# Two key products on VectorE and the slots' denominators on TensorE, in a four-layer graph kernel

## The chip, the core and the metric

One core of a Trainium2 chip runs the whole kernel. Its engines work side by side, each through its own queue in order: TensorE (PE, matrix products into PSUM), VectorE (DVE), ScalarE (ACT), GpSimd (POOL, which also issues the indirect DMAs here) and SyncE (SP, which issues the other DMAs). They wait for one another through semaphores. The metric is the device time of one execution in microseconds; shown times are medians of several runs.

## The reference, cut to what matters

Four layers over N = 2708 nodes with 128 channels, each added to its input after a layer norm and a ReLU. The change lies in layer 1, the attention:

```python
q = (x @ Wq.T).reshape(d, n, h)          # d = 128 slices, n = 2708 nodes, h = 8
k = (x @ Wk.T).reshape(d, n, h)
v = (x @ Wv.T).reshape(d, n, h)
a = jnp.einsum('dnh,dmh->dnm', q, k) * scale
a = a + spatial_encoding + edge_encoding   # both are adj: a sparse matrix, 1 to 16 entries in a row
a = jax.nn.softmax(a, axis=2)
out = jnp.einsum('dnm,dmh->dnh', a, v)
```

A softmax over all 2708 nodes, for each of 128 slices, with a sparse term added to the logits.

## The kernel before, in words

The kernel splits the softmax in two parts. **The dense part** is without adj: the exponential of a small logit is written as a cubic polynomial in the products of the eight coordinates of q and k, so that sums over all nodes become small matrix products of features. **The sparse part** is a correction for each node's neighbours, with weight exp(logit) times (exp(2 adj) - 1).

**Dense part.** Slices are taken in 64 pairs, d = 0 to 63, and each pair in six chunks of node tiles, c = 0 to 5 (`chunks`, L1515; 4, 4, 3, 4, 4 and 3 tiles of 22). In one pass of the loop over c (L1624):

- `turn` (L1519) transposes the query features of the next chunk on TensorE into `f_ps`, ScalarE copies them to `fT`.
- `evaluate` (L1530) multiplies them with the moments `mw` into `g_ps` on TensorE; VectorE multiplies by the last coordinates into `z` (L1546) and reduces into `o_raw` (L1555).
- `queries(d + 1)` makes the next pair's query features in `fq` on VectorE (L802, helper `mul_v`): p0, p1, p2 at c = 1, xy at c = 2, t0 and t1 at c = 3, t2 and the norms at c = 4.
- `moments(d + 1)` multiplies the key features `fk` with the values `y` on TensorE into `m_ps` (L869), c = 0 to 4; `weighted` (L877) makes `mw` of them at c = 5.
- `keys(d + 2)` makes key features in `fk` on GpSimd (L805, helper `mul_g`): p0, p1, p2 at c = 1, xy (16 products per node and slice) at c = 2, t0 (10 products) at c = 3, t1, t2 and the norms at c = 4. `with_values(d + 2)` multiplies keys with values into `y`, on GpSimd, at c = 3 and c = 5.

The query features read their coordinates from `kq_ps`, a copy in PSUM; the key features read `kv_t`, a copy in SBUF.

**Sparse part.** At the end of each pass the loop also advances a chain of generators, `first` (L1422): by slices, then sorting of the rows, then `from_neighbours` (L1211), in which nodes stand sorted by their number of neighbours in 22 tiles of 128, and tile t has `ROOM[t]` slots (16, 9, 8, ... 2; 121 in all). A slot b takes one neighbour of each of 128 nodes:

- `load`: an indirect DMA from GpSimd's queue gathers the neighbours' keys and values into `c_kv`, two slots ahead, in a ring of five buffers
- `logits` (L1246): GpSimd multiplies keys by queries, in place
- `summed` (L1252): VectorE reduces over the eight coordinates into `c_c`, in PSUM; two slots alternate in `c_two`
- `weigh` (L1258): ScalarE takes the exponential and scales by the weight, in place; for a tile's first slot it also copies the result to `c_den`
- `values` (L1269): VectorE multiplies values by weights into `c_v`; for later slots it then adds the weights to `c_den` (L1282)
- `added` (L1284): TensorE adds `c_v` into `v_ps` with two products by the identity
- `copied_out` (L1301), `store`: at a tile's end ScalarE copies sums and denominators out, and an indirect DMA stores them

`from_neighbours` yields six times per slot. In one round it does, with a yield between: load of slot b+2 and values of b-2; logits of b; summed of b-1; added of b-2; weigh of b-1; copied_out. `faster()` (L1417) sets four yields per chunk when this stage begins. So a pair (six chunks, 24 yields) takes exactly four slots, and the places where they fall into the six chunks are the same in every pair. The instructions are issued in the order in which the code runs (`manual_schedule`); only the waits are added by the framework.

After the stage the rest of `first` is gone, and the loop goes on with normalising and the output projection beside the remaining pairs.

Of the kernel before, what the change touches and what calls it, by code (L numbers as in the profile page):

```python
# [9 lines left out]
FP = mybir.dt.float32  # L10
AF = mybir.ActivationFunctionType
ALU = mybir.AluOpType
# [4 lines left out]
P = 128  # L17
BF = mybir.dt.bfloat16
BK = 512
HEAD = 8  # L20
# [7 lines left out]
ROOM = (16, 9, 8, 7, 7, 7, 6, 6, 6, 5, 5, 5, 5, 4, 4, 4, 4, 3, 3, 3, 2, 2)  # L28
# [10 lines left out]
LIN, XX, YY, XY, YYY, F_END = 1, 5, 15, 25, 41, 61  # L39
# [7 lines left out]
def gnn4_kernel(  # L47
# [22 lines left out]
    nc = tc.nc  # L70
    N, C = x.shape
# [19 lines left out]
    ident = const.tile([P, P], FP, name="ident")  # L91
# [114 lines left out]
    with ExitStack() as ph:  # L206
# [56 lines left out]
        with tc.manual_schedule():  # L263
# [108 lines left out]
            for i, t in enumerate(order):  # L372
                r0, sz = rows[t]
# [6 lines left out]
                d = dinv[:sz, t : t + 1]  # L380
# [100 lines left out]
            for t in range(STAY, NT):  # L481
# [3 lines left out]
                sz = rows[t][1]  # L485
# [78 lines left out]
    most2 = keep.tile([P, 2, C], FP, name="most2")  # L564
# [168 lines left out]
    parts = [(0, NT // 2), (NT // 2, NT)]  # L733
    TM = max(b - a for a, b in parts)

    def features(mul, k, k2, f, most):

        T = k.shape[1]
        n = k.shape[0]
        gs = k[:, :, :HEAD].rearrange("p t (g e) -> p t g e", g=2)  # L740
        hs = k2[:, :, :HEAD].rearrange("p t (g e) -> p t g e", g=2)
        two = f[:, :, XX : XX + 20].rearrange("p t (g w) -> p t g w", g=2)
        yy = f[:, :, YY : YY + 10]

        def pair(e, o):
            w = 3 - e
            mul(
                two[..., o : o + w],
                gs[..., e : e + 1].to_broadcast([n, T, 2, w]),
                hs[..., e + 1 : 4],  # L750
            )

        def triple(o, left, right):
            w, v = left.shape[2], right.shape[2]
            if v == 1:
                mul(f[:, :, o : o + w], left, right.to_broadcast([n, T, w]))
            else:
                mul(
                    f[:, :, o : o + w * v].rearrange("p t (a b) -> p t a b", a=v),
                    left[:, :, None].to_broadcast([n, T, v, w]),  # L760
                    right[:, :, :, None].to_broadcast([n, T, v, w]),
                )

        def norms_of():
            n2 = early.tile([P, 2 * NT], FP, name="n2", bufs=2)
            nc.vector.tensor_reduce(n2, two[..., 3:7], axis=AX.XY, op=ALU.add)
            nc.vector.tensor_reduce(
                most, n2.rearrange("p (t i) -> p i t", i=2), axis=AX.X, op=ALU.max
            )

        return {
            "sq": lambda: nc.scalar.activation(two[..., 3:7], gs, AF.Square),  # L772
            "lin": lambda: nc.scalar.copy(f[:, :, LIN : LIN + 4], k[:, :, 4:8]),
            "p0": lambda: pair(0, 0),
            "p1": lambda: pair(1, 7),
            "p2": lambda: pair(2, 9),
            "xy": lambda: triple(XY, k2[:, :, 0:4], k[:, :, 4:8]),
            "t0": lambda: triple(YYY, yy, k[:, :, 4:5]),
            "t1": lambda: triple(YYY + 10, yy[:, :, 4:], k[:, :, 5:6]),
            "t2": lambda: triple(YYY + 16, yy[:, :, 5:7], k[:, :, 6:8]),  # L780
            "n": norms_of,
        }
# [31 lines left out]
    fks, fqs, fts, pms, mws, ros = {}, {}, {}, {}, {}, {}  # L814

    copied, turned_ = {}, {}

    def of_pair(d, at):
        i = 2 * (d % (GRP // 2))
        return got[d // (GRP // 2)][:, i : i + 2, :, at]  # L820

    def flat(a):
        return a.rearrange("p t i k -> p (t i) k")
# [6 lines left out]
    def keys(d):  # L830

        kv = early.tile([P, NT, 2, QKV - HEAD], FP, name="kv_t", bufs=KV_BUFS)
        nc.scalar.copy(kv.rearrange("p t i k -> p i t k"), of_pair(d, slice(HEAD, QKV)))  # L833
        turned_[d] = kv = flat(kv)
        fks[d] = fkp[d % 2]
        return features(mul_g, kv, kv, flat(fks[d]), most2[:, 1, 2 * d : 2 * d + 2])

    def with_values(d, h):

# [52 lines left out]
    def opening():  # L892
# [23 lines left out]
        for part in (queries(0), keys(1)):  # L916
            yield from whole(part)
# [8 lines left out]
    with ExitStack() as ph:  # L926
# [10 lines left out]
        with tc.manual_schedule():  # L937
# [10 lines left out]
            for t, (r0, sz) in enumerate(rows):  # L948
# [4 lines left out]
                for i in range(3):  # L953
                    scale = (C**-0.5, 1.0, 1.0)[i]
                    for c0 in (0, HALF):
# [5 lines left out]
                            start=True,  # L961
                            stop=True,
# [112 lines left out]
    with ExitStack() as ph:  # L1075
# [3 lines left out]
        sm = ph.enter_context(tc.tile_pool(name="l1_sm", bufs=2, reuse_waits="tile"))  # L1079
# [5 lines left out]
        ps_c = ph.enter_context(tc.tile_pool(name="l1_psc", bufs=1, space=PSUM, reuse_waits="tile"))  # L1085
# [123 lines left out]
        S = 1  # L1209

        def from_neighbours():  # L1211
# [4 lines left out]
            nc.vector.tensor_scalar_add(cw, cw, -1.0)  # L1216
            todo = [(t, s0, w) for t in range(NT) for s0, w in _cuts(ROOM[t], S)]
            qs, kvs, cs, accs, dens = {}, {}, {}, {}, {}
            c_two = ps_c.tile([P, 2, S, C], FP, name="c_c")
            done = []  # L1220

            def load(b):
# [35 lines left out]
            def weigh(b):  # L1258

                t, s0, w = todo[b]  # L1260
                sz = rows[t][1]
                c = cs[b][:sz]
                nc.scalar.activation(c, c, AF.Exp)  # L1263
                nc.scalar.activation(c, c, AF.Copy, scale=cw[:sz, t, s0 : s0 + 1])
                if s0 == 0:
                    dens[t] = sm.tile([P, C], FP, name="c_den")
                    nc.scalar.copy(dens[t][:sz], c)

            def values(b):  # L1269
                t, s0, w = todo[b]  # L1270
                sz = rows[t][1]
                c, kv = cs.pop(b)[:sz], kvs.pop(b)
                vs[b] = z = tm.tile([P, 2, BK // HEAD, HEAD], FP, name="c_v", tag="c_v")
                nc.vector.tensor_tensor(  # L1274
                    z[:sz],
                    kv[:sz, 0, :, 1].rearrange("p (j c) k -> p j c k", j=2),
                    c.rearrange("p (j c) -> p j c", j=2)[:, :, :, None]
                    .to_broadcast([sz, 2, C // 2, HEAD]),
                    ALU.mult,
                )  # L1280
                if s0:
                    nc.vector.tensor_tensor(dens[t][:sz], dens[t][:sz], c, ALU.add)  # L1282

            def added(b):  # L1284
                t, s0, w = todo[b]
                sz = rows[t][1]
                z = vs.pop(b)
                if s0 == 0:
                    accs[t] = ps_v.tile([P, 2, BK], FP, name="v_ps")
                for j in range(2):  # L1290
                    nc.tensor.matmul(  # L1291
                        accs[t][:sz, j],
                        ident[:sz, :sz],
                        z[:sz, j].rearrange("p c k -> p (c k)"),
                        start=s0 == 0,
                        stop=s0 == ROOM[t] - 1,
                    )
                if s0 + w == ROOM[t]:
                    done.append(t)

            def copied_out():  # L1301
                while done:
                    t = done.pop()
                    sz = rows[t][1]
                    acc = nkv[t % 2].rearrange("p t c -> p (t c)")[:, : C * VW].rearrange(
                        "p (c k) -> p c k", k=VW
                    )
                    nc.scalar.copy(
                        acc[:sz, :, :HEAD],
                        accs.pop(t)[:sz].rearrange("p j (c k) -> p (j c) k", k=HEAD),  # L1310
                    )
                    nc.scalar.copy(acc[:sz, :, HEAD], dens.pop(t)[:sz])
                    ready.append((t, acc))

            def store():
# [47 lines left out]
        def unit_of(g):  # L1363
            return g // 2 if g < NG - 2 else g - NG // 2 + 1
# [52 lines left out]
        def faster():  # L1417

            pace[0] = 4.0
            yield  # L1420

        first = chain(by_node(), sorted_rows(), faster(), from_neighbours())  # L1422
        beside = []
        done = 0
# [34 lines left out]
            return ps_v.tile([P, 2, BK], FP, name="v_ps")  # L1459

        def sum_bank():
            return ps_c.tile([P, 2, S, C], FP, name="c_c")[:, 0, 0]

        def projected(t, ring):

# [148 lines left out]
        with tc.manual_schedule():  # L1614
# [7 lines left out]
            for d in range(D):  # L1622
                asked, keyed = {}, {}
                for c in range(NCH):  # L1624
# [32 lines left out]
                    while owed >= 1 and first is not None:  # L1657
                        owed -= 1
                        if next(first, "done") == "done":
                            first = None  # L1660
                    if first is None:
                        owed = 0
                        for _ in range(4):
                            step(n, unit_of(max((d - 1) // PG, 0)))
                        if d < D - 1:
                            normalising()
# [34 lines left out]
    with ExitStack() as ph:  # L1701
        with ExitStack() as gh:
# [7 lines left out]
            with tc.For_i(0, once):  # L1710
                with tc.For_i(0, C) as d:
# [5 lines left out]
                    q, k, v = nat  # L1717
# [5 lines left out]
                    o = gp.tile([P, NT, HEAD], FP, name="g_o")  # L1723
# [105 lines left out]
        with tc.tile_pool(name="l2_pa", bufs=1, space=PSUM) as pa, tc.manual_schedule():  # L1829
# [3 lines left out]
            for i, t in enumerate(in_turn):  # L1833
                sz = rows[t][1]
# [10 lines left out]
                for c, (c0, cw) in enumerate(cols):  # L1845
                    nc.tensor.matmul(
                        pgs[c][:, :cw], h2[:sz, t], a[:sz, c0 : c0 + cw],
                        start=i == 0, stop=i == NT - 1,
# [29 lines left out]
        with tc.tile_pool(name="l3_g4", bufs=NC) as g4, tc.tile_pool(  # L1878
            name="l3_ln", bufs=2, space=PSUM
# [121 lines left out]
    with ExitStack() as ph, tc.manual_schedule():  # L2001
        gp = ph.enter_context(tc.tile_pool(name="l3_g", bufs=4, reuse_waits="tile"))
        zp = ph.enter_context(tc.tile_pool(name="l3_z", bufs=2, reuse_waits="tile"))
        sm = ph.enter_context(tc.tile_pool(name="l3_sm", bufs=3))
# [58 lines left out]
    with tc.tile_pool(name="l3_more", bufs=2) as mp, tc.tile_pool(  # L2063
        name="l3_once", bufs=1
# [7 lines left out]
        with tc.For_i(0, nc.values_load(ovf, min_val=0, max_val=1)):  # L2072
# [13 lines left out]
            most = mp.tile([P, 1], FP, name="most")  # L2086
# [10 lines left out]
            with tc.For_i(0, rounds):  # L2097
                for t, (r0, sz) in enumerate(rows):
# [11 lines left out]
                    f = mp.tile([P, 8], FP, name="col_f")  # L2110
# [76 lines left out]
```

## Time and profile before

| | us |
|---|---|
| median of 3 runs (2151.46 to 2160.33) | 2151.55 |
| the profiled execution | 2157.09 |
| its span in the trace | 2155.3 |
| slots of neighbours, first load to last `v_ps` product | about 743 to 1471 |

Busy time over the whole span: TensorE 1692.6 us (79%), VectorE 1444.2 (67%), GpSimd 1321.0 (61%), ScalarE 931.8 (43%). These shares are means over stages with different limits; what the change is worth is read from the stage between 743 and 1471 us. In the trace a float32 product with 128 moving columns is recorded as two matmuls, so counts of products are half of the counts of records; transposes are recorded once.

### The profile page before, as it was taken

The numbers are of one execution on the slowest core, as the hardware profiler recorded it, in microseconds if no ns is written. First come the engines' busy times: TensorE is split into PE (matmuls) and PEld (weight loads), VectorE is DVE, ScalarE is ACT, GpSimd is POOL, SyncE is SP. The second block draws the span as 40 slices with busy tenths as digits, with TensorE's granted clock in tenths as the row PEclk, the third lists the DMA queues.
The fourth block names the chain that finished last, engine by engine and source line by source line (L and its number), as shares of the span: only waits on it lengthen the run. The fifth ranks groups of instructions, "written<-read, shape, count | busy, mean of one in ns | idle before, by whom it ended". The sixth has DMA issues, their size and how long they took to land. (4 is left out here: it accounts for less than half of the span.)

```text
span 2155.3 us, 30079 instructions
## 1 busy us (share of the span) xinstructions
PE 1692.6 (79%) x10634; PEld 1348.4 (63%) x10634; DVE 1444.2 (67%) x3232; ACT 931.8 (43%) x2049; POOL 1321.0 (61%) x1363
## 2 busy tenths in 40 slices
PE   4767989988889788988888888888889769943442
PEld 3656864488789666666666665667889745423431
DVE  6899846366677788888888888877788720134331
ACT  3947744376677444444444444444445210021010
POOL 1343332066566699999999999997667210057762
PEclk9978999999999999999999999988999979965555
DMA  4755319778799676667766766764767757433331
GB/s 158 298 164 191 134 57 363 294 246 249 240 300 318 177 245 239 225 238 255 252 231 240 237 244 245 250 237 143 228 202 223 242 152 276 155 138 104 94 100 38
DMA packets 256854, 453.68 MB, mean 210 GB/s; under 512 B 112267, under 2 KB 180110, under 8 KB 231483
## 3 DMA queue, kind: packets, MB, share of 16 engines
q1 hardware_dynamic: 225459, 282.79, 39.6%
q0 software_dynamic: 31232, 168.86, 23.0%
q8 instruction: 85, 1.39, 0.3%
q14 instruction: 78, 0.64, 0.1%
HBM read 336.99 MB, written 114.60 MB: 210 GB/s over the span
## 5 line engine op out<-in xcount | busy, mean ns | idle before, releaser
L1538 PE MATMUL g_ps<-mw,fT 128*124 128x124 f32 x2816 | 377.9, 277 | 10.8 <-DVE mw L883 6.2
L869 PE MATMUL m_ps<-y,fk 123*128 123x128 f32 (+1 forms) x2816 | 372.6, 278 | 0.2 <-POOL fk L805 0.2
L1538 PEld LDWEIGHTS g_ps<-mw,fT 128*124 128x124 f32 x2816 | 344.5, 192 | 12.0 <-DVE mw L883 7.1
L869 PEld LDWEIGHTS m_ps<-y,fk 123*128 123x128 f32 (+1 forms) x2816 | 345.6, 194 | 1.3 <-issue 1.0
L1528 ACT COPY fT<-f_ps 128x496 f32<-128x496 f32 (+1 forms) x384 | 208.6, 543 | 242.1 <-PE f_ps L1524 239.9
L1291 PE MATMUL v_ps<-c_v,ident 128*128 128x512 f32 (+1 forms) x484 | 254.3, 651 | 74.7 <-DVE c_v L1274 74.0
L805 POOL TENSOR_TENSOR fk<-kv_t 128x264 f32<-128x264 f32 (+3 forms) x256 | 188.5, 761 | 186.4 <-ACT kv_t L833 185.6
L1546 DVE TENSOR_TENSOR z<-g_ps,bq 124x360 f32<-124x360 f32 (+1 forms) x384 | 191.1, 498 | 163.3 <-PE g_ps L1538 151.0
L1524 PE MATMUL f_ps<-ident,fq 124*128 124x124 f32 x1408 | 222.9, 278 | 94.1 <-DVE fq L802 63.8
L1250 POOL TENSOR_TENSOR c_kv<-c_kv,c_q 128x1024 f32<-128x1024 f32 (+1 forms) x121 | 284.3, 2350 | 5.0 <-DMA c_kv<-kv_n,srt 3.4
L1524 PEld LDWEIGHTS f_ps<-ident,fq 124*128 124x128 f32 x1408 | 167.4, 145 | 188.5 <-issue 90.1
L805 POOL TENSOR_TENSOR y<-kv_t 128x704 f32<-128x704 f32 x128 | 191.0, 1492 | 67.6 <-PE m_ps L869 67.0
L1555 DVE TENSOR_REDUCE o_raw<-z 124x72 f32<-124x360 f32 (+1 forms) x384 | 190.7, 497 | 13.2
L1291 PEld LDWEIGHTS v_ps<-c_v,ident 128*128 128x128 f32 (+1 forms) x484 | 86.8, 200 | 151.7 <-DVE c_v L1274 69.2
L1256 DVE TENSOR_REDUCE c_c<-c_kv 128x128 f32<-128x1024 f32 (+1 forms) x121 | 148.0, 1223 | 50.2 <-POOL c_kv L1250 47.7
L1263 ACT ACTIVATE c_c<-c_c 128x128 f32<-128x128 f32 (+1 forms) x121 | 31.7, 262 | 330.6 <-DVE c_c L1256 312.9
L805 POOL TENSOR_TENSOR fk<-fk,kv_t 128x440 f32<-128x440 f32 (+2 forms) x192 | 154.9, 821 | 5.5 <-ACT fk L772 5.3
L1274 DVE TENSOR_TENSOR c_v<-c_kv,c_c 128x1024 f32<-128x1024 f32 (+1 forms) x121 | 146.6, 1211 | 0.0
L1235 POOL DMA_INDIRECT c_kv<-kv_n,srt x121 | 118.0, 975 | 22.3 <-issue 8.6
L1974 POOL DMA_INDIRECT g<-tab_d,l_nbr x99 | 103.5, 1045 | 30.2 <-issue 29.8
L957 PE MATMUL qkv_ps<-wT,hT 128*128 128x512 f32 (+1 forms) x264 | 116.9, 601 | 0.4 <-ACT hT L438 0.4
L170 POOL TENSOR_TENSOR n_hot<-n_hot,n_fl 128x640 f32<-128x640 f32 (+1 forms) x22 | 34.0, 1545 | 119.6 <-DVE n_hot L164 116.0
(315 smaller groups left out, 2989.0 us busy)
## 6 DMA issues: line engine op xcount, KB each, us to landing
a_nat<-in_adj_dram SPq DMA_DIRECT2D x34, 1354.0 KB
raw<-qkv_d SPq DMA_DIRECT2D x128, 275.0 KB
qkv_d<-qkv SPq DMA_DIRECT2D x21, 1600.0 KB
n_raw<-qkv_d SPq DMA_DIRECT2D x96, 275.0 KB
kv_n<-n_kv SPq DMA_DIRECT2D x16, 1408.0 KB
fk<-in_adj_dram SPq DMA_DIRECT2D x12, 1354.0 KB
o_g<-o_raw SPq DMA_DIRECT2D x31, 396.0 KB
fq<-in_adj_dram SPq DMA_DIRECT2D x9, 1354.0 KB
```

The costliest lines, as they stand in the source:

```text
L805: nc.gpsimd.tensor_tensor(o, x, y, ALU.mult)
L869: nc.tensor.matmul(pms[d][:, :P], fks[d][:sz, t].rearrange("p i f -> p (i f)"), wide[h][:sz, o : o + P], start=t == 0, stop=t == NT - 1,)
L1235: nc.gpsimd.indirect_dma_start(out=kvs[b][:sz, e].rearrange("p c e k -> p (c e k)"), out_offset=None, in_=kv_n.rearrange("n c k -> n (c k) ...
L1250: nc.gpsimd.tensor_tensor(k, k, qs[t][:sz], ALU.mult)
L1256: nc.vector.reduce_sum(cs[b][:sz], kvs[b][:sz, 0, :, 0], axis=AX.X)
L1274: nc.vector.tensor_tensor(z[:sz], kv[:sz, 0, :, 1].rearrange("p (j c) k -> p j c k", j=2), c.rearrange("p (j c) -> p j c", j=2)[:, :, :, None]
L1291: nc.tensor.matmul(accs[t][:sz, j], ident[:sz, :sz], z[:sz, j].rearrange("p c k -> p (c k)"), start=s0 == 0, stop=s0 == ROOM[t] - 1,)
L1524: nc.tensor.transpose(pt[:, m, :USED], fqs[d][:USED, t0 + m].rearrange("p i f -> p (i f)"), ident[:USED, :USED])
L1528: nc.scalar.copy(fts[d, c][:, :n, :USED], pt[:, :n, :USED])
L1538: nc.tensor.matmul(pg[:USED, m, :USED], ft[:, m, :USED], mws[d][:, :USED], start=True, stop=True,)
L1546: nc.vector.tensor_tensor(z[:USED, : 2 * n], pg[:USED, :n] .rearrange("p m (i w) -> p (m i) w", i=2)[:, :, : VW * B_ALL] .rearrange("p a ( ...
L1555: nc.vector.reduce_sum(ros[g][:USED, t0 : t0 + n, i : i + 2].rearrange("p m i k -> p m (i k)"), z[:USED, : 2 * n].rearrange("p (m i) k b - ...
```

## The change

Two edits, both in force only in the stage of slots.

**Key products.** `features` gets an argument `heavy`. With it, xy and t0 are multiplied by that helper; `keys` passes `mul_v` (VectorE) while the list `crowded` is filled. `faster()` fills it when the stage of slots begins, and it is emptied when `first` is done. The other key products stay on GpSimd. xy and t0 keep their places in the loop (c = 2 and c = 3).

**Denominators.** Each slot's weights are copied to an own `c_den` on ScalarE, and a product by the identity adds them up on TensorE in `added`, after the two products of that slot. The sum stands in two further parts of `c_two`, which grows from two to four parts of 128 columns; VectorE's addition goes away.

```diff
-    def features(mul, k, k2, f, most):
+    def features(mul, k, k2, f, most, heavy=None):
...
-            "xy": lambda: triple(XY, k2[:, :, 0:4], k[:, :, 4:8]),
-            "t0": lambda: triple(YYY, yy, k[:, :, 4:5]),
+            "xy": lambda: triple(XY, k2[:, :, 0:4], k[:, :, 4:8], heavy or mul),
+            "t0": lambda: triple(YYY, yy, k[:, :, 4:5], heavy or mul),
...
+    crowded = []
...
-        return features(mul_g, kv, kv, flat(fks[d]), most2[:, 1, 2 * d : 2 * d + 2])
+        return features(
+            mul_g, kv, kv, flat(fks[d]), most2[:, 1, 2 * d : 2 * d + 2],
+            mul_v if crowded else None,
+        )
...
-            c_two = ps_c.tile([P, 2, S, C], FP, name="c_c")
+            c_two = ps_c.tile([P, 4, S, C], FP, name="c_c")
...
                 nc.scalar.activation(c, c, AF.Copy, scale=cw[:sz, t, s0 : s0 + 1])
-                if s0 == 0:
-                    dens[t] = sm.tile([P, C], FP, name="c_den")
-                    nc.scalar.copy(dens[t][:sz], c)
+                dens[b] = sm.tile([P, C], FP, name="c_den", bufs=3)
+                nc.scalar.copy(dens[b][:sz], c)
...
-                if s0:
-                    nc.vector.tensor_tensor(dens[t][:sz], dens[t][:sz], c, ALU.add)
...
+                nc.tensor.matmul(
+                    c_two[:sz, 2 + t % 2, 0],
+                    ident[:sz, :sz],
+                    dens.pop(b)[:sz],
+                    start=s0 == 0,
+                    stop=s0 == ROOM[t] - 1,
+                )
...
-                    nc.scalar.copy(acc[:sz, :, HEAD], dens.pop(t)[:sz])
+                    nc.scalar.copy(acc[:sz, :, HEAD], c_two[:sz, 2 + t % 2, 0])
...
             pace[0] = 4.0
+            crowded.append(True)
...
-            return ps_c.tile([P, 2, S, C], FP, name="c_c")[:, 0, 0]
+            return ps_c.tile([P, 4, S, C], FP, name="c_c")[:, 0, 0]
...
                         if next(first, "done") == "done":
                             first = None
+                            crowded.clear()
```

More of the change, by code (lines that the diff above doesn't have):

```diff
@@ L751, in pair, with triple @@
             )
-        def triple(o, left, right):
+        def triple(o, left, right, mul=mul):
             w, v = left.shape[2], right.shape[2]
```

## The prediction

> **What bounds the kernel now.** First the busy shares of the stage that the change touches, from its first load to its last product (columns: stretch, length, then busy us of PE, PEld, DVE, ACT, POOL, and PE's clock):
>
> ```profile
> 743.00:1471.00 728.00, 621.78 (x3850) 466.18 (x3849) 608.25 (x1115) 315.79 (x827) 689.67 (x561) 0.96 0.68 240
> ```
>
> GpSimd is busy for 95%, TensorE for 85%, VectorE for 84%. Then the stage's groups of instructions, and who waited for whom, both from 800 to 1400 us:
>
> ```profile
> L1250 POOL TENSOR_TENSOR c_kv<-c_kv,c_q 128x1024 f32<-128x1024 f32 x101 | 237.4, 2351 | 1.3
> L1235 POOL DMA_INDIRECT c_kv<-kv_n,srt x102 | 99.6, 977 | 18.6 <-issue 7.1 <-POOL fk L805 3.2 <-POOL c_kv L1250 2.7
> L805 POOL TENSOR_TENSOR fk<-kv_t 128x704 f32<-128x704 f32 x25 | 36.7, 1470 | 0.5
> L805 POOL TENSOR_TENSOR fk<-fk,kv_t 128x440 f32<-128x440 f32 x25 | 26.4, 1058 | 0.0
> L802 DVE TENSOR_TENSOR fq<-bq,kq_ps 128x704 f32<-128x704 f32 x25 | 22.0, 878 | 0.0
> L802 DVE TENSOR_TENSOR fq<-fq,kq_ps 128x440 f32<-128x440 f32 x25 | 15.1, 606 | 0.0
> L1282 DVE TENSOR_TENSOR c_den<-c_den,c_c 128x128 f32<-128x128 f32 x84 | 23.5, 280 | 0.0
> ...
> DVE z L1546 <- PE g_ps L1538: 39.4, 37, 2.7
> DVE c_c L1256 <- POOL c_kv L1250: 36.5, 29, 3.0
> ```
>
> The reader sees that GpSimd's idle time is 0.2 us gaps at DMA issues: it waits for nobody and sets the pace. 121 slots with six yields, and three more rounds, are 31.2 pairs of four slots; 728 / 31.2 = 23.3 us a pair. GpSimd's xy products start 21.95, 23.2 or 24.5 us apart, by whether none, one or two of the tile's extra DMA issues (about 1.0 us each and a gap) fall into the pair.
>
> What would bind without GpSimd? The time line of one pair (start, us, engine):
>
> ```profile
> 1003.64 1.22 DVE L1256 TENSOR_REDUCE c_c<-c_kv 128x128 f32<-128x1024 f32 x1
> 1003.79 0.59 PE L1524 MATMUL f_ps<-ident,fq 124*128 124x124 f32 x4
> ...
> 1004.21 1.03 PE L1538 MATMUL g_ps<-mw,fT 128*124 128x124 f32 x8
> 1004.89 0.26 ACT L1263 ACTIVATE c_c<-c_c 128x128 f32<-128x128 f32 x1 [3.69 <-DVE c_c L1256]
> ...
> 1005.28 0.53 DVE L1546 TENSOR_TENSOR z<-g_ps,bq 124x360 f32<-124x360 f32 x1 [0.42 <-PE g_ps L1538]
> ```
>
> TensorE's f_ps and g_ps run while VectorE still reduces c_c, so z waits only 0.42 us. From the start of f_ps to z is 1.49 us. The sum of VectorE's steps (start to next start) over a pair is 20.0 us; with its short waits a pair in which GpSimd was not late took 21.72 us (xy of the queries at 1002.84, the next at 1024.56). This **VectorE-TensorE loop of 21.7 us** lies just under GpSimd's 23.3.
>
> **The change part by part.**
>
> *Off GpSimd:* xy and t0, 1.47 + 1.06 = 2.53 us a pair. It falls to 20.8 us. If nothing else happened, the loop would bind.
>
> *Onto VectorE:* xy at 0.88 and t0 at 0.61 by the queries' rows, 0.80 + 0.55 counted start to next start. c_den goes: four a pair, 0.20 us each from start to next start (1001.83 to 2.03), 0.80. Net +0.55 on the loop. The query rows read one operand from PSUM, the new ones both from SBUF; that is the second unknown below. t0 also waits for GpSimd's p0 to p2, issued two chunks earlier: no wait expected.
>
> *Onto TensorE:* 121 products of 128 columns, two records each. m_ps records of that size follow each other every 0.112 us, so 0.22 to 0.27 us each with the gap, 1.1 us a pair: 621.8 / 31.2 + 1.1 = 21.0 us. By itself hidden.
>
> *Onto ScalarE:* 99 copies at 0.265 us (as L1267's): 26 us beside 412 us of idle time in the stage. Hidden.
>
> *The new wait.* In the built changed program, in the issue order of chunk 2, PE's denominator product waits for VectorE's reduction of the **next** slot, and ScalarE's exp for that PE product instead of for the reduction (semaphore values traced to their setters; b counts slots):
>
> ```
> DVE  L1277 c_v  (b-2)
> DVE  L802  xy of the queries, xy of the keys
> DVE  L1260 c_c  (b-1)
> PE   L1292 v_ps (b-2) x2
> PE   L1299 c_c<-c_den (b-2)     waits DVE L1260 (b-1)
> PE   L1533 f_ps, L1547 g_ps     queued behind it
> ACT  L1267 exp (b-1)            waits PE L1299 (b-2)
> ```
>
> They touch different columns, but one tile. Here a rule speaks against the change: the Trainium skill's "PSUM — Partial Sum Buffer", section on bank collisions, has PSUM guarded by bank, not by address, for any two of TensorE, ScalarE and VectorE; four parts of 128 float32 fill one bank by that page's size of 2 KiB. No run here shows a collision; the trace shows only c_c shared by DVE and ACT in turn. By address alone the pair would take 21.72 + 0.55 = 22.3 us: (22.3 - 23.3) x 31.2 = -32 us. By the bank, with the waits as built:
>
> - **Chunk 2 to 3.** `added` stands right behind `summed`. c_c ends, 0.05 us to PE, 0.27 for the denominator, 1.49 from f_ps to z: z waits 1.81 us after c_c, now 0.42. +1.39.
> - **Chunk 5 to 0.** The same place, now 0.77 us (c_c ends 1016.18, z starts 1016.95): +1.04.
> - **Chunks 1 and 4.** `summed` was a chunk earlier, so PE doesn't wait. But exp, which started at 1020.72, must now follow v_ps (from 1019.73, 1.82 us) and the denominator: about 1021.85. Then `values` can start at about 1022.5, and in a pair that GpSimd doesn't delay VectorE wants it earlier. Bounds 0 and 0.7; I take 0.36 in chunk 1 (laying out a pair by hand), none in chunk 4, where the norms give 1.3 us of cover.
>
> Loop: 21.72 + 0.55 + 1.39 + 1.04 + 0.36 = **25.06 us**. VectorE is on this path all the time, apart from these waits, so every item counts in full. GpSimd at 20.8 and TensorE at 21.0 are no longer bounds.
>
> *The second unknown: two SBUF inputs.* A row of later in the trace has them (min/median/max ns):
>
> ```profile
> L1405 DVE TENSOR_TENSOR r_c<-r_o,r_rs x30: 878/916/3191, 1495.1 to 1732.5; 128x704 f32<-128x704 f32 x30
> L1170 DVE TENSOR_TENSOR s_four<-s_four,s_own x1: 5611/5611/5611, 724.3 to 724.3; 128x352 f32<-128x352 f32 x1
> ```
>
> The queries' xy of the same 704 elements, one input in PSUM, stays at 877 to 892. L1170 is 352 elements, elsewhere 0.52 us; it started at 724.32, when GpSimd had begun a run of products, and ended at 729.93, as that run did. The Trainium skill's "SBUF — State Buffer", section "Who interferes with whom", says it: a VectorE instruction with two SBUF inputs and a GpSimd instruction that reads SBUF exclude each other for the whole instruction. By the query rows keys' xy and t0 cost 1.35 us; by the rule up to a GpSimd run (2.35 + 1.28 = 3.6 us) more for each. L1405 means 1.338 us, 0.46 over its least: twice that is 0.9. In the new order GpSimd's next slot begins with a load, which waits for `values`; VectorE reaches xy 1.5 us after `values` ends, about when the load is over, and t0 when GpSimd has run dry. So I take 0.3 us a pair, ends 0 and 3.6.
>
> **Sum.** (25.06 + 0.3 - 23.3) x 31.2 = +64 us. The profiled execution took 2157.1 (span 2155.3), so it would be 2221; against the median, 5.5 us lower, **2215 us**. Before and after the stage nothing changes.
>
> **Rivals.**
>
> - *Relief.* The waits hide (VectorE's reductions come early, now that GpSimd isn't late) and the 2.53 us come through down to the loop without the waits: -32 us, 2120. It decides when the three waits together cost under 1.0 us a pair (23.3 - 22.3). For it: GpSimd is 95% busy and everyone else waits for it. Against: the denominator's wait names a reduction behind new VectorE work.
> - *Break-even.* PE's waits cost half (1.3 us) and the lock nothing: 21.72 + 0.55 + 1.3 = 23.6, +9 us, 2160. For it: L1291 already waits for c_v 65 us in 600, so TensorE has slack to lose; against: it is z's path that loses.
> - *The lock decides.* Slower by far: r_c comes in pairs, 1.69 us without delay, and 15 of them took 13.6 us more than that in all (0 to 3.6 each). If both products meet it so, 0.9 us each, 1.8 a pair stands in place of 0.3: +111 us, 2262. For it: VectorE reaches xy just as GpSimd's next product is due. Against: GpSimd now has spare time, in which VectorE finds the port free.
> - *Nothing moves.* Excluded: the built program has 62 rows fewer on GpSimd, 62 key products on VectorE and 121 products on TensorE.
>
> **How the numbers follow.** Forecast (2175 to 2250, between half of the lock's and chunk 1's ends and two thirds of the waits) 0.60; lock 0.18; relief 0.13; break-even 0.09, of which 0.05 within 0.5% (11 us, about what measuring this kernel can tell from no change) and 0.04 slower. Faster 0.13, same 0.05, slower 0.82. The range 2157 to 2265 leaves out relief and the worse part of the lock.
>
> **What would show it.** The stage lasts 780 to 800 us; GpSimd is busy for some 80% of it; PE waits at c_c L1299 for DVE L1260, ScalarE's exp for PE; z L1555 waits 60 us more or so for g_ps; VectorE's fk rows mean 0.9 and 0.6 us if the lock is light. I am wrong if z's waits stay as they are, or if fk on VectorE takes over 1.5 us.

## The result, and the profile after

| | before | after |
|---|---|---|
| median of four runs each, us | 2154.41 | 2278.45 (2266.11 to 2282.41) |
| ratio, 95% interval | | 1.056 (1.051 to 1.061) |
| profiled execution, us | 2157.09 | 2281.64 |
| stage of slots, first load to last `v_ps` product, us | 743.0 to 1472.9 (730) | 741.0 to 1601.5 (860) |

The change makes the kernel 5.6% slower: +124 us where +64 was forecast. It is all in the stage of slots (+131 us); what lies ahead of it and behind it lasts 6 us less than it did. First the busy time of the stage (columns: stretch, length, busy us of PE, PEld, DVE, ACT and POOL, PE's clock, DMA share and GB/s), then the same for 800 to 1400 us:

```profile
741.00:1601.50 860.50, 690.95 (x4111) 527.91 (x4111) 663.92 (x1076) 337.20 (x931) 626.64 (x501) 0.94 0.58 203
800.00:1400.00 600.00, 482.09 (x2883) 369.44 (x2881) 466.24 (x755) 232.20 (x647) 436.03 (x348) 0.95 0.57 202
```

GpSimd, which was busy for 95%, is now busy for 73%, VectorE for 77%, TensorE for 80%. No engine is full, and the stage is longer: engines wait for one another in turn. The groups of instructions (800 to 1400 us; total and mean ns, then idle time in front and its releasers):

```profile
L1254 POOL TENSOR_TENSOR c_kv<-c_kv,c_q 128x1024 f32<-128x1024 f32 x85 | 199.8, 2350 | 1.5
L1239 POOL DMA_INDIRECT c_kv<-kv_n,srt x86 | 88.2, 1026 | 89.6 <-DVE c_v L1277 67.3 <-DVE mw L887 10.4 <-issue 5.7
L802 DVE TENSOR_TENSOR fk<-kv_t 128x704 f32<-128x704 f32 x22 | 39.3, 1786 | 0.0
L802 DVE TENSOR_TENSOR fq<-bq,kq_ps 128x704 f32<-128x704 f32 x22 | 19.3, 879 | 0.0
L1299 PE MATMUL c_c<-c_den,ident 128*128 128x128 f32 x172 | 39.0, 311 | 64.1 <-DVE c_c L1260 64.1
```

In the same 600 us there are 85 slots' products on GpSimd instead of 101. It now waits in front of its loads, 67 us of it for VectorE's `c_v`. The keys' xy on VectorE has a mean of 1786 ns beside 879 for the queries' product of the same size. And the new product waits 64 us for VectorE's reduction. Who waited for whom, the first line before the change (there the exponential stands in L1263), the others after it (us in total, times, longest):

```profile
ACT c_c L1263 <- DVE c_c L1256: 259.8, 94, 4.1
...
ACT c_c L1267 <- PE c_c L1299: 320.4, 86, 8.8
...
DVE z L1555 <- PE g_ps L1547: 100.1, 43, 3.4
...
DVE c_v L1277 <- ACT c_den L1270: 9.5, 19, 0.5
```

Before, ScalarE's exponential waited for VectorE's reduction itself (260 us). Now it waits for a TensorE product of another slot. The wait that hurts most is that of z on VectorE: 39.4 us became 100.1. The time line of one pair shows how (start, length):

```profile
1019.26 0.89 DVE L802 TENSOR_TENSOR fk<-kv_t 128x704 f32<-128x704 f32 x1
...
1020.06 1.22 DVE L1260 TENSOR_REDUCE c_c<-c_kv 128x128 f32<-128x1024 f32 x1
...
1021.43 0.46 PE L1299 MATMUL c_c<-c_den,ident 128*128 128x128 f32 x2 [1.66 <-DVE c_c L1260]
1021.73 0.59 PE L1533 MATMUL f_ps<-ident,fq 124*128 124x124 f32 x4
1021.93 0.26 ACT L1267 ACTIVATE c_c<-c_c 128x128 f32<-128x128 f32 x1 [4.71 <-PE c_c L1299]
...
1023.22 0.53 DVE L1555 TENSOR_TENSOR z<-g_ps,bq 124x360 f32<-124x360 f32 x1 [1.94 <-PE g_ps L1547]
```

VectorE, TensorE, VectorE one behind the other: f_ps used to run while VectorE reduced, and now starts 0.45 us after the reduction has ended. Measured from one start of the queries' xy to the next, the shortest pairs, most of them without a tile's end, last 25.57 to 25.58 us; the others 26.3 to 32.6 us.

### The profile page after: what moved, and what is told of

Its sections match the earlier page's. It is cut to its first block, busy times and chain, and to the rows that moved or that the text cites. A ratio compares the mean times of both kernels' runs of the same rounds, so it can differ in the third digit from the quotient of the medians.

```text
span 2279.7 us, 30690 instructions
## 1 busy us (share of the span) xinstructions
PE 1760.0 (77%) x10876; PEld 1406.2 (62%) x10876; DVE 1502.6 (66%) x3195; ACT 950.2 (42%) x2148; POOL 1257.1 (55%) x1301
## 5 line engine op out<-in xcount | busy, mean ns | idle before, releaser
L1547 PE MATMUL g_ps<-mw,fT 128*124 128x124 f32 x2816 | 392.0, 283 | 10.4 <-DVE mw L887 5.4
L873 PE MATMUL m_ps<-y,fk 123*128 123x128 f32 (+1 forms) x2816 | 383.8, 283 | 0.0
L1547 PEld LDWEIGHTS g_ps<-mw,fT 128*124 128x124 f32 x2816 | 358.6, 199 | 11.5 <-DVE mw L887 6.3
L873 PEld LDWEIGHTS m_ps<-y,fk 123*128 123x128 f32 (+1 forms) x2816 | 357.9, 200 | 1.0 <-issue 1.0
L1292 PE MATMUL v_ps<-c_v,ident 128*128 128x512 f32 (+1 forms) x484 | 248.7, 638 | 68.6 <-DVE c_v L1277 67.3
L1533 PE MATMUL f_ps<-ident,fq 124*128 124x124 f32 x1408 | 229.6, 284 | 79.0 <-DVE fq L802 40.7
L805 POOL TENSOR_TENSOR fk<-kv_t 128x264 f32<-128x264 f32 (+3 forms) x225 | 143.8, 666 | 211.6 <-ACT kv_t L834 211.4
L1277 DVE TENSOR_TENSOR c_v<-c_kv,c_c 128x1024 f32<-128x1024 f32 (+1 forms) x121 | 147.1, 1216 | 33.5 <-ACT n_kv L1320 19.5
L1299 PEld LDWEIGHTS c_c<-c_den,ident 128*128 128x128 f32 (+1 forms) x242 | 44.1, 202 | 166.1 <-issue 155.8
L805 POOL TENSOR_TENSOR fk<-fk,kv_t 128x440 f32<-128x440 f32 (+2 forms) x161 | 122.5, 778 | 6.0 <-ACT fk L772 5.8
L1299 PE MATMUL c_c<-c_den,ident 128*128 128x128 f32 (+1 forms) x242 | 54.3, 308 | 85.5 <-DVE c_c L1260 85.5
```

The lines of the kernel that those rows point to most:

```text
L805: nc.gpsimd.tensor_tensor(o, x, y, ALU.mult)
L873: nc.tensor.matmul(pms[d][:, :P], fks[d][:sz, t].rearrange("p i f -> p (i f)"), wide[h][:sz, o : o + P], start=t == 0, stop=t == NT - 1,)
L1277: nc.vector.tensor_tensor(z[:sz], kv[:sz, 0, :, 1].rearrange("p (j c) k -> p j c k", j=2), c.rearrange("p (j c) -> p j c", j=2)[:, :, :, None]
L1292: nc.tensor.matmul(accs[t][:sz, j], ident[:sz, :sz], z[:sz, j].rearrange("p c k -> p (c k)"), start=s0 == 0, stop=s0 == ROOM[t] - 1,)
L1533: nc.tensor.transpose(pt[:, m, :USED], fqs[d][:USED, t0 + m].rearrange("p i f -> p (i f)"), ident[:USED, :USED])
L1547: nc.tensor.matmul(pg[:USED, m, :USED], ft[:, m, :USED], mws[d][:, :USED], start=True, stop=True,)
```

## The experiments

Three theories stood after this reading. **Bank:** the order that the semaphores make PE, DVE and ACT keep in `c_two`, which by the prediction's working now fills a bank, makes the loop longer. **Port:** the keys' products on VectorE, with both operands in SBUF, wait for GpSimd. **Added work:** the engines simply have more to do. The kernel before was run again on the same chip in each group of runs: 2156.8 us beside the first four, 2158.9 beside the next four, 2144.3 beside the last three. Ratios are to that one.

### One part of the change at a time

`keys_only` has the key products on VectorE and the denominators as before; `den_only` the reverse.

```diff
 keys_only:
-                dens[b] = sm.tile([P, C], FP, name="c_den", bufs=3)
+                if s0 == 0:
+                    dens[t] = sm.tile([P, C], FP, name="c_den")
...
 den_only:
-            mul_v if crowded else None,
+            None,
```

> Only the key products move to VectorE; denominators as before. Bank theory with the measured port delay: VectorE's loop 21.72 + 1.35 = 23.1 us a pair and about 0.9 for the port, so 24.0 against 23.3: 2165 to 2190 us. Port theory (it causes most of the loss): 2230 or more. If GpSimd's relief comes through: under 2145.

> Only the denominators move to TensorE; key products stay on GpSimd. Bank theory: the loop is 25.6 - 1.35 = 24.2 us a pair plus about 0.9 at tile ends, over GpSimd's 23.3: 2190 to 2225 us. Port theory: no instruction with two SBUF inputs is left, so as before, 2145 to 2165.

| | us | ratio (95%) | pair without a tile's end |
|---|---|---|---|
| keys_only | 2180.98 | 1.012 (1.010 to 1.014) | 22.9 to 23.0 |
| den_only | 2195.87 | 1.019 (1.017 to 1.022) | 24.25 |
| both (the change) | 2278.45 | 1.056 (1.051 to 1.061) | 25.57 |

Each half alone is slower, by 24 and 39 us, and together they cost 124, twice the sum of 63. The loop explains this. It took 21.72 us before, under GpSimd's 23.3, so that 1.6 us a pair of loss cost nothing. `den_only` takes off 0.80 us of VectorE's work and comes out at 24.25: its waits are worth 24.25 - (21.72 - 0.80) = 3.33 us a pair. Adding the two key products, 1.35 us, gives 25.60; the change has 25.57. On the loop of a plain pair the parts do add; against the time before they don't, since each alone uses up the same 1.6 us of slack (about 50 us in 31.2 pairs). 24 + 39 + 50 is 113 of the 124 us. The plain pairs of `keys_only`, 22.9 us, are not longer than before; its 24 us come from the others, in which xy waits for GpSimd.

### Take the bank and the port away

`elsewhere` adds the denominators into columns of `v_ps`, a tile of its own, instead of `c_two`; the work stays, but the sums written out are not the reference's. `psum_side` leaves the bank shared and lets xy and t0 of the keys read one operand from `kq_ps`: the durations of two products with one PSUM input, but products of other numbers. `both_gone` does both.

```diff
 elsewhere:
                 nc.tensor.matmul(
-                    c_two[:sz, 2 + t % 2, 0],
+                    accs[t][:sz, 1, :C],
                     ident[:sz, :sz],
                     dens.pop(b)[:sz],
-                    start=s0 == 0,
+                    start=False,
...
 psum_side (hk: the queries' copy in kq_ps):
-            "xy": lambda: triple(XY, k2[:, :, 0:4], k[:, :, 4:8], heavy or mul),
-            "t0": lambda: triple(YYY, yy, k[:, :, 4:5], heavy or mul),
+            "xy": lambda: triple(XY, (k2 if hk is None else hk)[:, :, 0:4], k[:, :, 4:8], heavy or mul),
+            "t0": lambda: triple(YYY, yy, (k if hk is None else hk)[:, :, 4:5], heavy or mul),
```

> The whole change, but the denominator's product adds into columns of v_ps, a bank that VectorE's slot reductions don't touch; the denominators are then not the reference's. Same instructions, same engines. Bank theory: the product no longer waits for the next slot's reduction and exp no longer for the product, so the pair falls from 25.6 us (plain) to about 22.5, GpSimd's 20.8 below it; with some 0.9 us a pair for the port the stage is near that of before: 2150 to 2185 us. Rival (it is the added work on VectorE, TensorE and ScalarE, wherever the sum stands): 2260 to 2280. Rival (the shared SBUF port causes most of it): over 2230.

> The whole change, but the two key products on VectorE read one operand from the queries' copy in PSUM (so they compute other products). Same sizes and places, one SBUF input each. The trace of the changed kernel shows 26.5 us for xy and 2.7 us for t0 over their undelayed durations in the stage. Bank theory: these 29 us go, 2240 to 2260. Port theory (delays also throw the phases off, most of the loss hangs on it): under 2210. If the port only takes time that would be waited anyway: 2270 to 2280.

> The denominators' product in the bank of v_ps (not the reference's denominators) and the keys' xy and t0 with one operand from the queries' copy in PSUM (other products), so that neither the shared bank nor the port is left. If these two are the whole loss: a plain pair of 22.4 us by the loop of VectorE and TensorE, 2120-2145 us, faster than before. If something third costs time (the load that waits for values, the tile ends): 2150 us or more.

Microseconds over the kernel before on the same chip (time, and the 95% interval of the ratio):

| | port in dispute | port free |
|---|---|---|
| bank shared | +124 (the change) | +77 (`psum_side`, 2233.91; 1.034 to 1.040) |
| bank not shared | +16 (`elsewhere`, 2172.62; 1.005 to 1.010) | **-37** (`both_gone`, 2121.92; 0.982 to 0.985) |

The four fields are almost a sum: the bank costs 114 us with the port free and 108 with it in dispute, the port 53 and 47. With both gone the same work is faster than before, so "added work" falls, and no third cost is left once these two are gone. "Bank" is short for more than one thing here: tile and bank change together in these runs, and the waits are semaphores that the framework set. Whether it set them for the tile or for the bank, and what a second tile in the same bank would cost, no run separates.

`psum_side` was expected at 2240 to 2260, by the 29 us that VectorE's records show beyond the undelayed length; the port takes some 18 us more than that. (In `elsewhere` the records show 58 us of delay, and the port costs 53.) TensorE's clock goes with it: the clock granted from 800 to 1400 us is 0.95 in the change and 0.99 in `psum_side`, 0.97 in `elsewhere` and 1.00 in `both_gone` (0.97 before). Over the stage, one minus the granted clock, times the length, is 53 us in the change and 15 us in `psum_side`. If half of these 38 us of lost clock lengthens the pairs, that is the 18 us; the half is an estimate, from two pairs of `end_sbuf` below.

`both_gone` by stretch, and its keys' xy (minimum, median, maximum in ns), where that of the change has 884/887/4764:

```profile
800.00:1400.00 600.00, 554.19 (x3598) 434.31 (x3597) 552.68 (x942) 299.21 (x820) 541.21 (x440) 1.00 0.73 256
```

```profile
L802 DVE TENSOR_TENSOR fk<-kq_ps,kv_t x31: 884/885/887, 775.1 to 1446.4; 128x704 f32<-128x704 f32 x31
```

VectorE and TensorE are both busy for 92%. All 26 pairs between 800 and 1400 us last 22.29 to 22.38 us, tile ends included: the prediction had this loop at 21.72 + 0.55.

What the port does is best seen in one place of the changed kernel, at the end of a tile:

```profile
988.58 2.33 POOL L1254 TENSOR_TENSOR c_kv<-c_kv,c_q 128x1024 f32<-128x1024 f32 x1
...
989.61 3.48 DVE L802 TENSOR_TENSOR fk<-kv_t 128x704 f32<-128x704 f32 x1
990.86 1.47 POOL L805 TENSOR_TENSOR y<-kv_t 128x704 f32<-128x704 f32 x1
...
994.37 0.77 PE L1299 MATMUL c_c<-c_den,ident 128*128 128x128 f32 x2 [4.25 <-DVE c_c L1260]
994.93 1.03 PE L1533 MATMUL f_ps<-ident,fq 124*128 124x124 f32 x4
```

```profile
994.36:997.77 3.41, 3.40 (x16) 3.41 (x17) 0.12 (x1) 1.88 (x6) 3.25 (x4) 0.50 0.86 308
```

xy of the keys starts while a GpSimd product runs, waits to its end, and waits through the next one too, which starts the moment the first ends: it is over 0.76 us after `y` is. This is no single case: in the stage 14 of the 31 xy last over 0.95 us, and each of them ends 0.75 to 0.76 us after a GpSimd product does. TensorE, whose next product waits for the reduction behind xy, stands still for 4.25 us, and then runs for 3.4 us at a granted clock of 0.50 (the second view; PE's clock is the third number from the end): f_ps takes 1.03 us, in the pair shown earlier 0.59.

### Move the product, and spare the bank at a tile's end

```diff
 den_early:
                 yield
+                if 0 <= b - 2 < M:
+                    counted(b - 2)      # the product, out of added(b - 2)
                 if 0 <= b - 1 < M:
                     summed(b - 1)
...
 end_sbuf (leaves the denominators out of the result):
-                    nc.scalar.copy(acc[:sz, :, HEAD], c_two[:sz, 2 + t % 2, 0])
+                    nc.scalar.copy(acc[:sz, :, HEAD], ones[:sz])
```

> The denominator's product of slot b-2 stands just before the reduction of slot b-1 instead of behind it, in the same bank. Bank theory (the time comes from the order of PE, DVE and ACT through one bank): f_ps no longer stands behind the next slot's reduction, so z's wait for g_ps falls from 1.94 us towards 0.4 us and a plain pair from 25.6 to 23.5-24.5 us; in all 2200-2230 us. 'It is only the added work on VectorE and TensorE': unchanged, 2265-2285 us.

> At a tile's end ScalarE copies a constant from SBUF instead of the denominators out of the shared bank; the denominators are left out of the output. If the read at the tile's end holds up VectorE (V waits for n_kv 19.5 us in 17 places, more_n on GpSimd later by as much): 15 to 30 us under the changed kernel, 2250-2265 us. If these waits only stand in place of others: within 6 us of it.

Both missed. `den_early` took 2290.17 us, 1.059 (1.057 to 1.062): not better than the change. Its waits (800 to 1400 us):

```profile
PE c_c L1305 <- DVE c_v L1277: 114.5, 50, 6.5
...
DVE z L1561 <- PE g_ps L1553: 68.0, 71, 1.5
```

z does wait less for g_ps (68 us instead of 100), but the product now waits for `c_v` of its own slot, 114 us, and holds f_ps up behind it. All 31 xy of the keys now run into a GpSimd product and last 1.31 us or more, and the clock granted from 800 to 1400 us, 0.91, is the lowest of all runs. Another place in the order exchanges the waits through the bank; it doesn't remove them.

`end_sbuf` took 2271.92, 1.053 (1.051 to 1.055). Its interval overlaps that of the change, so in the time nothing is gained that these runs can tell. Its pairs tell more. In the change `c_v` waits for ScalarE's reading of the denominators, 19.5 us in the stage and 12.0 between 800 and 1400 us (the first line below). This wait is gone, and the pairs with a tile's end in which the keys' products aren't late and the granted clock is 1.00 last 25.50 to 25.58 us, as those without one. With the bank shared and the port free (`psum_side`) most of them last 26.3 to 26.8. So this reading out of the shared bank is what a tile's end cost. Part of the gain went to the port: the median of xy of the keys is 1337 ns (the second line, of `end_sbuf`) instead of 887, and the delays of xy and t0 add up to 38 us in the stage instead of 29.

```profile
DVE c_v L1277 <- ACT n_kv L1320: 12.0, 10, 1.7
...
L802 DVE TENSOR_TENSOR fk<-kv_t x31: 885/1337/4606, 770.1 to 1590.7; 128x704 f32<-128x704 f32 x31
```

Two of these pairs also show the clock's share. In the pair that starts at 1176 us the keys' products are 1.27 us late, the granted clock is 1.00, and the pair is 1.25 us longer than 25.57. In the one at 1092 us they are 1.25 us late, 1.71 us of clock are lost, and the pair is 2.12 us longer: half of the lost clock comes on top.

### A smaller move

If the bank and the port are the price, the move of a key product can be had without them. t0 of the keys multiplies features by one coordinate. `t0_sbuf` moves t0 alone to VectorE. `t0_psum` also has ScalarE copy that coordinate into the unused ninth column of `kq_ps`, so that one operand is in PSUM. `t0_warm` is `t0_psum` with a product of zeros for each slot into `v_ps`; `before_warm` is the kernel before with the same product.

```diff
 t0_psum, in keys (t0 then reads last in place of k[:, :, 4:5]):
+        if crowded:
+            last = copied[d - 1][:, :, HEAD : HEAD + 1]
+            nc.scalar.copy(last, kv[:, :, 4:5])
...
 t0_warm and before_warm, in added:
+                nc.tensor.matmul(
+                    accs[t][:sz, 1, :C], ident[:sz, :sz], zc[:sz],
+                    start=False, stop=s0 == ROOM[t] - 1,
+                )
```

> The kernel before, with t0 of the keys alone on VectorE in the stage, and its one-coordinate operand copied into the unused ninth column of the queries' copy in PSUM; the reference's result in full. By the loops: GpSimd 23.3 - 1.06 = 22.2 us a pair, VectorE 21.72 + 0.55 = 22.3 us, the port not in dispute: 2120-2140 us, the best so far. If GpSimd's time can't be relieved without VectorE losing as much: 2150-2165 us.

> t0 of the keys on VectorE as in t0_psum, and one product of zeros more for each slot on TensorE, into v_ps (it adds nothing to the result). In t0_psum the pairs went from 22.2 to 23.7-24.2 us where v_ps of the slot at 11.3 us of the pair took 3.6 instead of 1.98 us. If that is a clock lost for want of work on TensorE: v_ps stays at 1.9-2.0 us, all pairs at 22.2-22.5 us, 2118-2130 us, and the times of single runs stand within some 8 us, not 32. If the slow v_ps has another cause: 2145-2175 us, with the same spread.

> The kernel before with the same product of zeros for each slot, and nothing moved. GpSimd sets its pace (95% busy), so a better clock on TensorE should bring little: 2145-2160 us by the reading that the clock only matters once GpSimd is relieved; 2130 us or less if the clock was what held up before.

> The kernel before with t0 of the keys alone on VectorE in the stage, both operands in SBUF. If the port shared with GpSimd delays t0 (as it did in keys_only): fk of 440 elements has a mean of 0.8 us or more instead of 0.605, with single ones of 2 us and above, and the time is above that of t0_psum, 2160-2175 us. If the port hardly matters for one product: as t0_psum, 2140-2165 us.

| | us (lowest to highest) | ratio (95%) |
|---|---|---|
| t0_sbuf | 2158.84 (2155.24 to 2162.77) | 1.007 (1.006 to 1.009) |
| t0_psum | 2154.03 (2134.28 to 2166.68, 20 runs) | 0.997 (0.995 to 1.000) |
| t0_warm | 2131.96 (2125.72 to 2135.88) | **0.994** (0.993 to 0.996) |
| before_warm | 2152.82 (2143.59 to 2155.30) | 1.003 (1.002 to 1.005) |

`t0_sbuf` shows the port again. Its fk of 440 elements has a mean of 1929 ns, over three times the 604 of `t0_psum` (743 to 1471 us), and a move that relieves GpSimd makes the kernel slower:

```profile
L802 DVE TENSOR_TENSOR fk<-fk,kv_t 128x440 f32<-128x440 f32 x29 | 55.9, 1929 | 0.0
...
L802 DVE TENSOR_TENSOR fk<-fk,kq_ps 128x440 f32<-128x440 f32 x30 | 18.1, 604 | 0.0
```

`t0_psum` missed its expectation, and its runs stand 32 us apart. In its trace the pairs last 22.2 to 22.5 us from 769 to 925 us and nearly all 23.7 to 24.2 from 994 us on. First a row of a short pair, then PE's rows of a long one and the z behind them, then the busy time of two stretches of the long one:

```profile
802.74 1.98 PE L1299 MATMUL v_ps<-c_v,ident 128*128 128x512 f32 x4 [1.08 <-DVE c_v L1282]
...
1002.67 0.61 PE L1533 MATMUL f_ps<-ident,fq 124*128 124x124 f32 x4 [0.87 <-DVE fq L802]
1003.12 0.81 PE L1547 MATMUL g_ps<-mw,fT 128*124 128x124 f32 x6
...
1005.02 3.68 PE L1299 MATMUL v_ps<-c_v,ident 128*128 128x512 f32 x4 [1.08 <-DVE c_v L1282]
...
1010.03 0.53 DVE L1555 TENSOR_TENSOR z<-g_ps,bq 124x360 f32<-124x360 f32 x1 [2.46 <-PE g_ps L1547]
```

```profile
998.20:1004.40 6.20, 4.79 (x28) 3.13 (x27) 6.01 (x12) 1.75 (x6) 5.72 (x5) 1.00 0.47 147
1004.40:1010.60 6.20, 5.58 (x23) 3.47 (x24) 3.63 (x9) 2.08 (x6) 6.02 (x6) 0.72 0.80 291
```

The four v_ps matmuls, 1.98 us in the short pair, take 3.68: TensorE runs at half its clock for 3.4 us after a stretch with little work, z is 2 us late, and the pair 1.5 us longer; the next pair repeats it. The Trainium skill's "TensorE: Matmul & The Clock Gate", Part 1 on the clock gate, has the clock halved after a window of some 3.4 us in which TensorE is idle. The halving agrees with this row; but TensorE was busy for 1.3 of the 3.2 us ahead of it and its longest gap was 1.1 us, so that here a thin stretch was enough.

With the product of zeros v_ps takes over 2.4 us in 5 of the 121 slots instead of 22, and the runs stand 10 us apart, as the clock theory has it. In time the zeros bring little: 0.994 against 0.997, and these two, taken on different chips, have intervals that touch. The usual pair is 22.7 us, not 22.2 to 22.5 as expected, probably because the product also stands in front of f_ps; and the time expected, 2118 to 2130, was missed by 2 us. `before_warm` is no faster than before, although the same slow slots fall from 13 to 5: there the clock is not what matters. `t0_warm` computes the reference's result in full and is the fastest complete kernel here, 0.6% under before.

## Why the prediction fell short

The direction and the two mechanisms were right, the sizes were not: the time, 2278, lies above the range's end of 2265. Of the 60 us that were missing, 38 are the port, put at 9 us where it costs 47, and 22 the bank's waits.

- **Off GpSimd, onto VectorE, by address alone** (20.8 us; 21.72 + 0.55 = 22.3 us a pair, -32 us): right. `both_gone`, which has just this, shows 22.3 us and -37.
- **The bank's waits** (25.06 us a pair, +55 us without the port): right in place, too small by 22 us (`psum_side`: +77). The pair is 25.57. z waits 1.94 us in chunks 3 and 0 where 1.81 was worked out, twice 0.13 (0.15 us from the reduction to PE where 0.05 was taken). The wait of `c_v` in chunk 1, taken as 0.36 between 0 and 0.7, is 0.53 us, and its releaser is the copy to `c_den`, a third ScalarE access to the bank that I hadn't counted beside the exponential and the scaling. These make 0.43 of the 0.51 us, and 0.51 x 31.2 is 16 us. The sum had no term for tile ends, at which ScalarE reads the denominators out of the shared bank: 0.7 to 1.2 us in most pairs that have one. 16 us and these are together more than 22; 31.2 equal pairs is a rough count, for the first pairs of the stage are shorter.
- **The port** (0.3 us a pair, +9 us): this is the step that failed. It costs 47 us, 1.5 us a pair. The argument that VectorE finds GpSimd at its load, or with time to spare, holds in the plain pairs (887 ns in the median) and fails at tile ends: there the store waits for ScalarE's `n_kv`, GpSimd's later product falls onto xy, and xy waits through up to two products. I had judged the pair by one layout, where 22 tile ends in 31 pairs shift it. Nor had the sum a term for the clock that TensorE loses behind such a wait.
- **ScalarE and TensorE hidden:** right for their own time; not for the place of their work in the bank.
- **Rivals.** Relief at 2120 is what the change would have given without bank and port (2122). "The lock decides" had a port of 1.8 us a pair, near the 1.5 measured, and was taken as a case of its own, at 2262; with the bank's waits too small as well, the range ended too low for both.

What was said to show it came so: PE waits at L1299 for the reduction, the exponential for PE, and z's waits grew by 61 us between 800 and 1400 us and by 89 in the stage (60 were named, for no stretch). The stage lasts 860 us instead of 780 to 800, and GpSimd is busy for 73% of it instead of 80. The named sign of being wrong, fk above 1.5 us, came too: 1786 ns.

## What to carry to other kernels

Before work moves to an idle engine, write down which PSUM tile and bank it reads and writes and who else uses them: here each further access from another engine joined the queue of the others. An engine that is 95% busy hides a loop just under it, so that two halves of 24 and 39 us made a change of 124; add them on the loop. Judge a port or lock by the pairs with irregular events, not by the plain ones.

## What was not expected of the hardware

A VectorE product with two SBUF inputs waited through two back-to-back GpSimd products (3.48 us in place of 0.885; up to 4.76), and with one input in PSUM it kept to 883 to 889 ns beside a busy GpSimd. And TensorE's clock can tip within one run: the same pair in `t0_psum` lasts 22.24 or 23.7 us, the long one without a gap over 1.1 us ahead of the slow matmuls, and with a product of zeros for each slot 5 slots are slow instead of 22.
